# Two network layers on one core: the second tile's mask and exponentials a step earlier, both scalings in one step, and a new order at the seams

## The chip, the core and the metric

The kernel runs on one core of a Trainium2 chip. Its engines are TensorE (PE, matrix products), VectorE (DVE), ScalarE (ACT), GpSimd (POOL) and SyncE (SP, which here issues every DMA). The metric is the device time of one execution in microseconds; lower is better. Each engine works through its own instructions in the order in which the program gives them, and waits on semaphores where an instruction needs another engine's result or a buffer that another engine still reads.

## The reference

Input are 128 graphs of 64 nodes with 768 features each (`x`) and their adjacency (`adj`). Two layers follow each other, each with a residual and a layer norm. Cut to what matters:

```python
# layer 0, 12 heads of 64
h = einsum('bnd,ade->bane', x, W);  th = tanh(h)
attn = (th . w_src) + transpose(th . w_dst)
attn = where(attn >= 0, attn, 0.2 * attn)
attn = softmax(where(~adj, -999.0, attn))
f = elu(attn @ h + b)
g = sigmoid(x @ H_w.T + H_b)
x = layernorm(x + g * f + (1 - g) * x)
# layer 1, 6 heads of 128
q, k, v = x @ Wq + bq, x @ Wk + bk, x @ Wv + bv
p = softmax(where(adj, q @ k.T / sqrt(128), -9e15))
x = layernorm(x + (p @ v) @ Wf + bf)
```

Everything is in 32-bit floats.

## The kernel before, in words

The 8192 rows are 64 tiles of 128 rows (two graphs each), and two tiles make a pair; there are 32 pairs. **Phase A** computes layer 0 and the V product of layer 1; **phase B** computes Q, K, the attention and the output product of layer 1, for 16 groups of two pairs. Nothing is left to a scheduler: both phases collect closures in a table `events` with `at(step, ...)`, and `run` calls them step by step. A step is therefore a place in the order of every engine, not a time. Within a step the closures stand in the order in which they were entered: older pairs first, and within a pair tile 1 before tile 0.

**The products of phase A.** Each product of a pair (`W`, `G` for the gate, `V`) is done in seven steps with pre-added blocks in place of eight (class `Product`, `mms` at L209); a step is three products of 128x128 by 128x384, which PE runs as six instructions. The blocks of the weights are added once (L173 and L167), those of the tokens for each pair on POOL (`token_sums`, L258 to L261) after DVE has transposed the tiles (`turn`, L395). Steps 0, 2 and 3 leave a snapshot of a PSUM bank in SBUF on ACT (`snap`, L416), since the bank goes on being accumulated: step 2 adds to the bank of step 0, step 4 to that of step 2, step 5 to that of step 3. Steps 1, 4 and 5 are taken out on DVE by an addition with a snapshot (L439 for W and G, L458 for V), step 6 by a copy on ACT (L437, L456). Step 6 adds to the bank that step 4's addition has read. In the steady part a pair `p` begins at step `o = 21 p - 21`: W at `o` to `o + 6`, G at `o + 7` to `o + 13`, and at `o + 14` to `o + 20` the V product of pair `p - 3`.

**A tile of layer 0** (class `Tile0`; the profile's lines are given). Tile 1 counts its steps from `s = o`, tile 0 from `s = o + 5`.

- `tanh` (ACT L475) and `cap`; `dst_mul` and `src_mul` (POOL L479, L487); `dst_sum` (DVE L482 and a transpose L484) and `src_sum` (DVE L491).
- `dst_out` (four DMAs, L497) writes the sums to DRAM, and `dst_in` (two DMAs, L505) reads them back spread over the partitions, into `s`. `exchange` (L515, L516) swaps halves of `h`.
- `add`: twelve Prelus on ACT (L529), in two halves. `mask` (DVE L536) and `top` (a maximum, DVE L540). `exp`: twelve exponentials on ACT with their sums (L545), in two halves.
- `scale`: per half a reciprocal on DVE (L553) and a product on POOL (L555).
- `probs`: six transposes on PE (L566) in two halves, each copied by ACT into `pt` (L571). `aggregate`: PE L584. `elu`: DVE L605, then `e` on ACT (L612), in a second use of the buffer `pt`.
- `mix1`, `mix2`: DVE L616, L617, L625, L626. `norm1`: statistics on DVE (L284, L293, L295), a power and two small products on POOL (L296, L298, L299). `norm2`: one pass on ACT (L303). `spill`: a DMA.
- `gate_in` (POOL L594) and `gate` (ACT L598) work on the gate.

**The end of phase A.** The last pair starts at `o = O[-1]`. No W or G follows it; the V products of pairs 29, 30 and 31 stand at `o + 21`, `o + 28` and `o + 45`. The last needs both tiles of pair 31 transposed, which PE does at `o + 42` and `o + 43` (L410, copies L411). Phase B's first weights are loaded from `o + 7` on; the 14 sums of the blocks of `Wq` run on POOL, one a step from `o + 22`, and those of `Wk` on DVE from `o + 36` (L167).

**Phase B.** A product over a group takes 15 steps (table `STEPS`, class `Stream`), each of two products of 128 by 128 by 256 (L866). They need eleven sums of token blocks (`group_sum`, L836, list `SUMS`; `SUM_STEPS` tells at which step each is used). The results accumulate through first copies on ACT (L887) and additions on DVE (L892 for q and k, L909 for the output product). A sum that names an index of 6 or more uses an earlier sum. For group 0 all sums stand ahead of its first product, two of three on DVE and the third on POOL; for group 1 every second one is on DVE; later groups have them on POOL.

**The end of the kernel.** The last pair's output gets its statistics by block (`end_stats`, L1039); `end_norm` then does for tile 1, and after it for tile 0: L1043 and L1045 on DVE, the power on POOL (L1046), two passes on DVE (L1049) each followed by a store (L1050).

Of the kernel before, what the change touches and what calls it, by code (L numbers as in the profile page):

```python
# [9 lines left out]
F32 = mybir.dt.float32  # L10
U8 = mybir.dt.uint8
AF = mybir.ActivationFunctionType
ALU = mybir.AluOpType
# [48 lines left out]
def kernel(  # L62
# [221 lines left out]
        nc.vector.bn_stats(st[:, half, :], r[:, halves(half)])  # L284
        return st

    def layernorm(small, r, eps):
        st = layernorm_half(small, r, None, 0)
        return layernorm_rest(small, layernorm_half(small, r, st, 1), eps)

    def layernorm_rest(small, st, eps):
        mv = small.tile([P, 2], F32, name="mv")
        nc.vector.bn_aggr(mv, st.rearrange("p a s -> p (a s)"))  # L293
        rstd = small.tile([P, 1], F32, name="rstd")
        nc.vector.tensor_scalar_add(rstd, mv[:, 1:2], eps)  # L295
        nc.gpsimd.tensor_tensor(rstd, rstd, neg_half, ALU.pow)  # L296
        shift = small.tile([P, 1], F32, name="shift")
        nc.gpsimd.tensor_tensor(shift, mv[:, 0:1], rstd, ALU.mult)  # L298
        nc.gpsimd.tensor_tensor(shift, shift, neg_one, ALU.mult)  # L299
        return rstd, shift  # L300

    def normalize(r, rstd, shift):
        nc.scalar.activation(r, r, AF.Identity, bias=shift, scale=rstd)  # L303


    def phase_a(ctx):
# [160 lines left out]
        class Tile0:  # L467
            def __init__(self, p, i):
                self.p, self.i, self.d = p, i, st[p]
                self.sd = sds[i]  # L470

            def tanh(self):
                self.h = self.d["h"][self.i]
# [126 lines left out]
            def elu(self):  # L600

                self.z = k3.tile([P, D], F32, name="z")
                zv = self.z.rearrange("p (j h e) -> p j h e", h=2, e=E)
                for h2 in range(2):
                    nc.vector.tensor_tensor(  # L605
                        zv[:, :, h2, :],
                        self.pos[h2],
                        b_bc[:, None, :].to_broadcast([P, A // 2, E]),
                        ALU.add,
                    )  # L610
                self.e = k3.tile([P, D], F32, name="pt")
                nc.scalar.activation(self.e, self.z, AF.Exp, bias=neg_one)  # L612

            def mix1(self):
# [11 lines left out]
                nc.vector.scalar_tensor_tensor(xt, xt, 4.0, e, op0=ALU.mult, op1=ALU.add)  # L626

            def norm1(self):
                self.stats = layernorm(small, self.d["x"][self.i], 4.0 * EPS)

            def norm2(self):
                xt = self.d["x"][self.i]
                normalize(xt, *self.stats)

            def spill(self):
# [30 lines left out]
        for p in range(NP):  # L666
            d, o = st[p], O[p]
            d["p"] = p
            if p:
                at(max(o - 20, 1), lambda p=p: load_adj(p))  # L670
                at(o + 8, lambda p=p: load(p))

            def xb_in(d, i):
                d.setdefault("xp", []).append(blocks(x_t[2 * d["p"] + i]))

            def xT(d, i):
                d.setdefault("T", []).append(turn(d["xp"][i]))

            if p:
                at(max(o - 20, 1), lambda d=d: xb_in(d, 0))  # L680
                at(max(o - 16, 1), lambda d=d: xb_in(d, 1))
                at(o - 6, lambda d=d: xT(d, 0))
                at(o - 5, lambda d=d: xT(d, 1))
                at(o - 4, lambda d=d: sums(d))
            else:
                at(0, lambda d=d: d.update(T=[transposed(t) for t in d["x"]]))
                at(0, lambda d=d: sums(d))
            at(o, lambda d=d: start_h(d))
            at(o + 7, lambda d=d: start_g(d))
            for i in range(7):  # L690
                at(o + i, lambda d=d, i=i: dense(d, "W", i))
                at(o + 7 + i, lambda d=d, i=i: dense(d, "G", i))
            for i, s in ((1, o), (0, o + 5)):
                t = Tile0(p, i)
                at(s + 6 + (i == 0), t.tanh, t.cap)
                at(s + 7, t.dst_mul)
                at(s + 8, t.src_mul)
                at(s + 9, t.dst_sum, t.dst_out)
                at(s + 10, t.src_sum)
                at(s + 13, t.dst_in)  # L700
                at(s + 16, t.exchange)

                at(s + (15 if i else 17), lambda t=t: t.add(0))
                at(s + (16 if i else 17), lambda t=t: t.add(1))
                at(o + (14 if i else 16), t.gate_in)
                at(o + (17 if i else 18), t.gate)
                at(s + 18, t.mask, t.top)
                at(s + 19, lambda t=t: t.exp(0))

                at(s + (19 if i else 20), lambda t=t: t.exp(1))  # L710
                at(s + 21, lambda t=t: t.scale(0))
                at(s + 22, lambda t=t: t.scale(1))
                at(s + 24, t.probs)
                at(s + 25, t.aggregate)
                at(s + 26, t.elu)
                at(s + 27, t.mix1)
                at(s + 28, t.mix2)
                at(s + 29, t.norm1)
                at(s + 30, t.norm2)
                at(s + 31, t.spill)  # L720

            def x1_in(d, i):
                d["xp", i] = blocks(x1_d[2 * d["p"] + i])

            def x1T(d, i, t):
                d["x1T", i] = t
                nc.sync.dma_start(xT_d[d["p"]][:, i], t)

            def x1_sums(d):
                d["T"] = [d["x1T", i] for i in range(2)]  # L730
                sums(d)

            if p < NP - 3:
                v = O[p + 3] + 14
                times = ((1, v - 19, v - 13), (0, v - 16, v - 10))
            elif p < NP - 1:

                v = O[-1] + (21 if p == NP - 3 else 28)
                times = ((1, v - 16, v - 7), (0, v - 15, v - 6)) if p == NP - 3 else (
                    (1, v - 12, v - 7), (0, v - 10, v - 6)  # L740
                )
            if p < NP - 1:
                for i, t0, t1 in times:
                    at(t0, lambda d=d, i=i: x1_in(d, i))
                    at(t1, lambda d=d, i=i: x1T(d, i, turn(d["xp", i])))
                at(times[1][2] + 1, lambda d=d: x1_sums(d))
            else:
                v = o + 45
                for i in range(2):
                    at(o + 43 - i, lambda d=d, i=i: x1T(d, i, transposed(d["x"][i])))  # L750
                at(o + 44, lambda d=d: x1_sums(d))
            at(v, lambda d=d: start_v(d))
            for i in range(7):
                at(v + i, lambda d=d, i=i: dense(d, "V", i))
# [14 lines left out]
            at(o + (7 + k if k < 4 else 8 + 2 * k), lambda k=k: load_early(0, Wq, k))  # L769
            at(o + 20 + 2 * k, lambda k=k: load_early(1, Wk, k))  # L770
        for k in range(len(WEIGHT_SUMS)):
            at(o + 22 + k, lambda k=k: weight15_sum(early[0], k, nc.gpsimd))
            at(o + 36 + k, lambda k=k: weight15_sum(early[1], k, nc.vector))
        at(o + 30, lambda: load_T4(0))
        run(events, O[-1] + 80)
# [3 lines left out]
    def phase_b(ctx, wq, wk):  # L779
# [258 lines left out]
                d["e", i] = k1.tile([P, 3, 6], F32, name=f"est{i}")  # L1038
            nc.vector.bn_stats(d["e", i][:, nb], d["x", 1, i][:, nb * 256 : (nb + 1) * 256])  # L1039

        def end_norm(g, d, i):
            mv = small.tile([P, 2], F32, name="mv")
            nc.vector.bn_aggr(mv, d["e", i].rearrange("p a s -> p (a s)"))  # L1043
            rstd = small.tile([P, 1], F32, name="rstd")
            nc.vector.tensor_scalar_add(rstd, mv[:, 1:2], EPS)  # L1045
            nc.gpsimd.tensor_tensor(rstd, rstd, neg_half, ALU.pow)  # L1046
            for half in range(2):
                r = d["x", 1, i][:, halves(half)]
                nc.vector.tensor_scalar(r, r, mv[:, 0:1], rstd, op0=ALU.subtract, op1=ALU.mult)  # L1049
                nc.sync.dma_start(out_t[4 * g + 2 + i][:, halves(half)], r)  # L1050
# [17 lines left out]
        for g in range(NG):  # L1068
# [6 lines left out]
            ready = {}  # L1075
            for k in range(len(SUMS)):

                eng = nc.vector if (k % 3 != 2 if g == 0 else g == 1 and k % 2) else nc.gpsimd
                if g == 0:
                    group_sum(d, k, eng)  # L1080
                    continue
                if g == 1:

                    t = max([R * 3 + SUM_STEPS[k] + 1] + [ready[r] for r in SUMS[k][:2] if r in ready])
                    ready[6 + k] = t
                else:
                    t = o - 24 + 2 * k
                at(t, lambda d=d, k=k, eng=eng: group_sum(d, k, eng))
# [15 lines left out]
            for q in range(2):  # L1104
# [37 lines left out]
                    at_first(f + i, lambda d=d, q=q, i=i: d["F", q].step(i))  # L1142
                if last and q:
                    for b in range(6):
                        t = f + 1 + max(i for i in range(R) if STEPS[i][5][b])
                        at(t, lambda d=d, b=b: end_stats(d, b))
                    for i in (1, 0):
                        at(f + R, lambda g=g, d=d, i=i: end_norm(g, d, i))
                    continue
                for i in range(2):  # L1150
                    t = f + R + 1 + 2 * i
# [48 lines left out]
```

## Time and profile before

| | |
|---|---|
| device time, median of 3 runs | 2919.01 us (2911.96 to 2919.04) |
| the profiled execution | 2916.2 us |
| its span | 2914.4 us |
| PE, PEld, DVE, ACT, POOL busy | 97, 71, 62, 41, 53% of the span |
| first matmul after | 5.99 us |
| phase A's last product ends, phase B's first begins | about 1510 us |
| granted clock of PE, mean | 0.995 |

A row of a timeline gives start and length in us, engine, line, operation, output and inputs, how many instructions were merged, and in brackets the idle time before it with what ended it. A row of the waits gives who waited for whom, the total in us, how often, and the longest wait. Times are from the start of the span. Ends of matmuls are modelled, so the distance between starts says more than the length of a row.

### The profile page before, as it was taken

The numbers are of one execution on the slowest core, as the hardware profiler recorded it, in microseconds if no ns is written. First come the engines' busy times: TensorE is split into PE (matmuls) and PEld (weight loads), VectorE is DVE, ScalarE is ACT, GpSimd is POOL, SyncE is SP. The second block draws the span as 40 slices with busy tenths as digits, with TensorE's granted clock in tenths as the row PEclk, the third lists the DMA queues.
The fourth block names the chain that finished last, engine by engine and source line by source line (L and its number), as shares of the span: only waits on it lengthen the run. The fifth ranks groups of instructions, "written<-read, shape, count | busy, mean of one in ns | idle before, by whom it ended". The sixth has DMA issues, their size and how long they took to land.

```text
span 2914.4 us, 50727 instructions
## 1 busy us (share of the span) xinstructions
PE 2838.2 (97%) x18108; PEld 2062.3 (71%) x18108; DVE 1820.1 (62%) x3710; ACT 1203.7 (41%) x3739; POOL 1554.4 (53%) x1641
## 2 busy tenths in 40 slices
PE   8899999999999999999989999999999999999998
PEld 4455555555555555555558888888888888888887
DVE  4876766767667677676775555555555555555556
ACT  3666566565665656656532212222211222211223
POOL 3755555556555555555563554455454455454455
PEclk9999999999999999999999999999999999999999
DMA  6434344453443544435560212122212212212222
GB/s 167 112 109 142 119 139 134 123 151 116 140 131 118 152 121 136 136 119 145 160 201 27 71 61 77 62 82 88 73 59 77 80 64 88 83 57 69 88 82 71
DMA packets 358683, 308.40 MB, mean 106 GB/s; under 512 B 226592, under 2 KB 304160, under 8 KB 358432
## 3 DMA queue, kind: packets, MB, share of 16 engines
q1 hardware_dynamic: 358432, 305.16, 34.1%
q8 instruction: 144, 2.36, 0.3%
q14 instruction: 107, 0.88, 0.1%
HBM read 191.41 MB, written 101.06 MB: 100 GB/s over the span
## 4 chain that ended last, share of the span: by engine, by line
PE 74%; ACT 10%; DVE 9%; POOL 4%; issue 2%; DMA 1%; SPq 1%; DVEq 0%; ACTq 0%; POOLq 0%
PE X L866 42%; PE X L209 25%; ACT s L545 4%; PE pb L1006 2%; POOL s L555 2%; DVE s L536 2%; ACT s L529 2%; PE pa L584 2%; PE pb L931 2%; ACT snap L416 1%; PE pa L566 1%; DVE pt L616 1%; DVE pt L617 1%; ACT pt L612 1%; DVE nmx L540 1%
## 5 line engine op out<-in xcount | busy, mean ns | idle before, releaser
L209 PE MATMUL X<-w,S 128*128 128x384 f32 x2304 | 799.2, 492 | 26.4 <-ACT snap L416 14.9
L866 PE MATMUL X<-S,w 128*128 128x256 f32 x2816 | 665.1, 382 | 3.7 <-DVE q L892 2.4
L209 PEld LDWEIGHTS X<-w,S 128*128 128x128 f32 x2304 | 428.0, 190 | 322.7 <-issue 30.8
L209 PE MATMUL X<-w,T 128*128 128x384 f32 x1728 | 600.8, 491 | 4.4 <-DMA w<-in_L_gnn_W_dram 2.5
L866 PEld LDWEIGHTS X<-S,w 128*128 128x128 f32 x2816 | 524.8, 190 | 76.8 <-DVE q L892 2.8
L209 PEld LDWEIGHTS X<-w,T 128*128 128x128 f32 x1728 | 328.9, 192 | 229.8 <-ACT snap L416 8.5
L848 POOL TENSOR_TENSOR Sc<-cT 128x256 f32<-128x256 f32 x224 | 161.6, 728 | 405.1 <-PE X L866 388.1
L866 PE MATMUL X<-w,Sc 128*128 128x256 f32 x1408 | 322.5, 381 | 1.0 <-DVE xs L909 0.8
L909 DVE TENSOR_TENSOR xs<-xs,X 128x256 f32<-128x256 f32 x512 | 210.8, 420 | 169.6 <-PE X L866 160.9
L545 ACT ACTIVATE s<-s,nmx 128x64 f32<-128x64 f32 x768 | 256.1, 335 | 128.4 <-DVE nmx L540 128.4
L866 PEld LDWEIGHTS X<-w,Sc 128*128 128x128 f32 x1408 | 265.5, 190 | 38.6 <-DVE xs L909 1.6
L892 DVE TENSOR_TENSOR k<-k,X 128x256 f32<-128x256 f32 x320 | 133.6, 421 | 217.8 <-PE X L866 167.6
L555 POOL TENSOR_TENSOR s<-s,rs 128x384 f32<-128x384 f32 x128 | 128.5, 1004 | 225.2 <-DVE rs L553 122.2
L892 DVE TENSOR_TENSOR q<-q,X 128x256 f32<-128x256 f32 x320 | 133.3, 420 | 184.0 <-PE X L866 149.3
L866 PE MATMUL X<-xb,w 128*128 128x256 f32 x960 | 236.6, 379 | 0.0
L303 ACT ACTIVATE xs<-xs,shift,rstd 128x768 f32<-128x768 f32 x62 | 63.5, 1025 | 417.8 <-POOL shift L299 409.7
L887 ACT ACTIVATE k<-X,bk_c 128x256 f32<-128x256 f32 x192 | 91.0, 474 | 304.5 <-PE X L866 304.5
L887 ACT ACTIVATE q<-X,bq_c 128x256 f32<-128x256 f32 x192 | 91.1, 474 | 282.5 <-PE X L866 282.5
L416 ACT COPY snap<-X 128x384 f32<-128x384 f32 x288 | 136.3, 473 | 172.8 <-PE X L209 170.8
L479 POOL TENSOR_TENSOR tmp<-th,wd_bc 128x768 f32<-128x768 f32 x64 | 137.6, 2150 | 122.6 <-ACT th L475 122.6
L866 PEld LDWEIGHTS X<-xb,w 128*128 128x128 f32 x960 | 181.2, 190 | 24.0
L529 ACT ACTIVATE s<-s,src 128x64 f32<-128x64 f32 x768 | 193.5, 339 | 4.8 <-DMA s<-dst_d 4.8
(118 smaller groups left out, 4026.4 us busy)
## 6 DMA issues: line engine op xcount, KB each, us to landing
xb<-in_x_dram SPq DMA_DIRECT2D x64, 384.0 KB
s<-dst_d SPq DMA_DIRECT2D x128, 192.0 KB
x_d<-xb SPq DMA_DIRECT2D x64, 384.0 KB
xT_d<-T SPq DMA_DIRECT2D x64, 384.0 KB
v_d<-v SPq DMA_DIRECT2D x128, 192.0 KB
xb<-xT_d SPq DMA_DIRECT2D x32, 768.0 KB
xb<-v_d SPq DMA_DIRECT2D x256, 96.0 KB
xs<-x_d SPq DMA_DIRECT2D x64, 384.0 KB
```

The lines of the kernel that those rows point to most:

```text
L209: nc.tensor.matmul(o, self.lhsT(i, c), rhs, start=first and c == 0, stop=last and c == CH - 1, skip_group_check=True,)
L303: nc.scalar.activation(r, r, AF.Identity, bias=shift, scale=rstd)
L416: nc.scalar.copy(t, ps)
L479: nc.gpsimd.tensor_tensor(self.tmp, self.th, wd_bc, ALU.mult)
L529: nc.scalar.activation(self.s[:, a], self.s[:, a], AF.Prelu, bias=self.src[:, a : a + 1], alpha=LEAKY_ALPHA,)
L545: nc.scalar.activation(self.s[:, a], self.s[:, a], AF.Exp, bias=self.nmx[:, a : a + 1], accum_out=self.sm[:, a : a + 1],)
L555: nc.gpsimd.tensor_tensor(t, t, rs[:, :, None].to_broadcast([P, A // 2, S]), ALU.mult)
L848: nc.gpsimd.tensor_tensor(t, pair_part(d, q, r0), pair_part(d, q, r1), op)
L866: nc.tensor.matmul(ps, self.lhsT(r, slot, c), self.rhs(r, slot, c), start=start and c == 0, stop=stop and c == 1, skip_group_check=True,)
L887: nc.scalar.activation(o[:, b], ps, AF.Identity, bias=bias[:, hd : hd + 1], scale=1.0 if positive else -1.0)
L892: nc.vector.tensor_tensor(o[:, b], o[:, b], ps, ALU.add if positive else ALU.subtract)
L909: nc.vector.tensor_tensor(o, o, ps, ALU.add if positive else ALU.subtract)
```

## The change

Seven edits, all in the order of the work or in where it is done.

1. Tile 1's `mask`, `top` and first half of `exp` stand one step earlier in all pairs (`n = s - 1`; the second half keeps its step). Tile 0 keeps its steps.
2. `scale(0)` and `scale(1)` stand in one step, for both tiles.
3. In the last pair tile 0 counts from `o + 3`, not `o + 5`.
4. In the last pair `e` uses the buffers `th` and `tmp`, not `pt`, and `norm2` is one pass on DVE with mean and power, in place of two small products on POOL and a pass on ACT.
5. The 14 sums of the `Wq` blocks stand two a step from `o + 21`.
6. Group 0's sums are all on DVE; the first four stand ahead of the products, the others up to four steps ahead of their use. In group 1 other six sums are on DVE, so that no sum on DVE needs one from POOL.
7. At the end the statistics stand a step earlier, and the first part of `end_norm` becomes `end_top`, which is done for both tiles before the passes, tile 1's a step before tile 0's.

```diff
-    def layernorm_rest(small, st, eps):
+    def layernorm_rest(small, st, eps, plain=False):
         mv = small.tile([P, 2], F32, name="mv")
         nc.vector.bn_aggr(mv, st.rearrange("p a s -> p (a s)"))
         rstd = small.tile([P, 1], F32, name="rstd")
         nc.vector.tensor_scalar_add(rstd, mv[:, 1:2], eps)
         nc.gpsimd.tensor_tensor(rstd, rstd, neg_half, ALU.pow)
+        if plain:
+            return mv[:, 0:1], rstd
...
+                self.last = p == NP - 1
...
-                self.e = k3.tile([P, D], F32, name="pt")
+
+                self.e = k3.tile([P, D], F32, name=("th", "tmp")[self.i] if self.last else "pt")
...
             def norm2(self):
                 xt = self.d["x"][self.i]
+                if self.last:
+                    mean, rstd = self.stats
+                    nc.vector.tensor_scalar(
+                        xt, xt, mean, rstd, op0=ALU.subtract, op1=ALU.mult
+                    )
+                    return
                 normalize(xt, *self.stats)
...
-            for i, s in ((1, o), (0, o + 5)):
+            for i, s in ((1, o), (0, o + (3 if p == NP - 1 else 5))):
...
-                at(s + 18, t.mask, t.top)
-                at(s + 19, lambda t=t: t.exp(0))
-
-                at(s + (19 if i else 20), lambda t=t: t.exp(1))
-                at(s + 21, lambda t=t: t.scale(0))
-                at(s + 22, lambda t=t: t.scale(1))
+                n = s - (i == 1)
+                at(n + 18, t.mask, t.top)
+                at(n + 19, lambda t=t: t.exp(0))
+                at(n + 20, lambda t=t: t.exp(1))
+                at(s + 21, lambda t=t: t.scale(0), lambda t=t: t.scale(1))
...
-            at(o + 22 + k, lambda k=k: weight15_sum(early[0], k, nc.gpsimd))
+            at(o + 21 + k // 2, lambda k=k: weight15_sum(early[0], k, nc.gpsimd))
...
-        def end_norm(g, d, i):
+        def end_top(d, i):
...
+            d["n", 1, i] = mv, rstd
+
+        def end_norm(g, d, i):
+            mv, rstd = d["n", 1, i]
...
-                eng = nc.vector if (k % 3 != 2 if g == 0 else g == 1 and k % 2) else nc.gpsimd
+
+                eng = nc.vector if g == 1 and k in (2, 3, 5, 6, 8, 10) else nc.gpsimd
                 if g == 0:
-                    group_sum(d, k, eng)
+
+                    t = max(min(SUM_STEPS[k], *(
+                        [SUM_STEPS[m] - 1 for m in range(len(SUMS)) if 6 + k in SUMS[m][:2]] or [99]
+                    )) - 4, -1)
+                    if t < 0:
+                        group_sum(d, k, nc.vector)
+                    else:
+                        at(t, lambda d=d, k=k: group_sum(d, k, nc.vector))
                     continue
...
-                        t = f + 1 + max(i for i in range(R) if STEPS[i][5][b])
+                        t = f + max(i for i in range(R) if STEPS[i][5][b])
                         at(t, lambda d=d, b=b: end_stats(d, b))
-                    for i in (1, 0):
-                        at(f + R, lambda g=g, d=d, i=i: end_norm(g, d, i))
+
+                    at(f + R - 2, lambda d=d: end_top(d, 1))
+                    at(f + R - 1, lambda d=d: end_top(d, 0))
+                    at(f + R - 1, lambda g=g, d=d: end_norm(g, d, 1))
+                    at(f + R - 1, lambda g=g, d=d: end_norm(g, d, 0))
```

More of the change, by code (lines that the diff above doesn't have):

```diff
@@ L285, in layernorm_half, with layernorm @@
         return st
-    def layernorm(small, r, eps):
+    def layernorm(small, r, eps, plain=False):
         st = layernorm_half(small, r, None, 0)
-        return layernorm_rest(small, layernorm_half(small, r, st, 1), eps)
-    def layernorm_rest(small, st, eps):
+        return layernorm_rest(small, layernorm_half(small, r, st, 1), eps, plain)
+    def layernorm_rest(small, st, eps, plain=False):
         mv = small.tile([P, 2], F32, name="mv")
@@ L628, in norm1 @@
             def norm1(self):
-                self.stats = layernorm(small, self.d["x"][self.i], 4.0 * EPS)
+                self.stats = layernorm(small, self.d["x"][self.i], 4.0 * EPS, self.last)
             def norm2(self):
                 xt = self.d["x"][self.i]
+                if self.last:
[4 more added lines that the diff above has]
+                    return
                 normalize(xt, *self.stats)
```

## The prediction

> **What bounds the kernel now.** I read the page's parts 1 and 2, then the table of stages, the waits and the timelines of single engines. Busy time, and TensorE's (PE's) share of each of 40 slices (72.9 us each):
>
> ```profile
> PE 2838.2 (97%) x18108; PEld 2062.3 (71%) x18108; DVE 1820.1 (62%) x3710; ACT 1203.7 (41%) x3739; POOL 1554.4 (53%) x1641
> PE   8899999999999999999989999999999999999998
> ```
>
> PE is full except at the start, at slice 20 (the seam between the phases) and at the end. By stage (us, PE, PEld, DVE, ACT, POOL busy, clock, DMA):
>
> ```profile
> 200.00:1430.00 1230.00, 1209.89 (x6392) 719.54 (x6391) 863.59 (x1417) 746.57 (x2599) 700.22 (x655) 1.00 0.45 132
> 1430.00:1600.00 170.00, 155.20 (x918) 114.32 (x917) 105.54 (x186) 56.60 (x156) 86.58 (x75) 0.98 0.40 127
> 1600.00:2880.00 1280.00, 1279.82 (x9804) 1108.26 (x9803) 697.62 (x1845) 286.51 (x595) 637.48 (x781) 1.00 0.22 73
> 2880.00:2915.00 35.00, 25.59 (x160) 21.35 (x158) 21.93 (x63) 4.48 (x5) 18.21 (x31) 0.93 0.25 90
> ```
>
> Phase B from 1600 on idles 0.2 us: nothing is to be had there. Steady phase A idles 20 us, the seam 15, the end 9. All of steady phase A's waits of PE (200 to 1430 us; total, times, longest):
>
> ```profile
> PE X L209 <- ACT snap L416: 11.4, 27, 0.4
> PE pa L566 <- POOL s L555: 8.7, 28, 0.3
> ```
>
> Two waits, once in each pair of tiles. One pair, PE first, then who is late:
>
> ```profile
> 819.29 4.03 PE L209 MATMUL X<-w,T 128*128 128x384 f32 x12
> 823.75 2.17 PE L209 MATMUL X<-w,S 128*128 128x384 f32 x6 [0.43 <-ACT snap L416]
> 837.15 0.49 PE L566 MATMUL pa<-ident,s 128*128 128x128 f32 x3
> 837.96 0.55 PE L566 MATMUL pa<-ident,s 128*128 128x128 f32 x3 [0.31 <-POOL s L555]
> ```
> ```profile
> 816.17 1.53 DVE L536 TENSOR_TENSOR s<-s,cap 128x768 f32<-128x768 f32 x1
> 823.14 0.47 ACT L416 COPY snap<-X 128x384 f32<-128x384 f32 x1
> 836.06 0.18 DVE L553 RECIPROCAL rs<-sm 128x6 f32<-128x6 f32 x1
> 836.38 1.52 POOL L555 TENSOR_TENSOR s<-s,rs 128x384 f32<-128x384 f32 x1 [2.22 <-DVE cap L522]
> ```
>
> A matmul of 384 columns starts every 0.3225 us (18 from 809.62 to 815.42). Twelve from 819.29 end at 823.16; the next starts at 823.75, 0.59 late, and its six take 0.07 longer: **0.66 us** for a shown wait of 0.43, since the pipeline empties. Likewise three transposes at 0.109 end at 837.48, and the next starts at 837.96: **0.48**. The first is W's step 2, waiting for the snapshot of step 0, which stands on ACT behind tile 1's 12 exponentials (818.78 to 822.78). The second waits for scale(1) of tile 0, whose reciprocal stands on DVE behind mix1. A pair takes 45.26 us (823.75 to 869.01).
>
> **What the Trainium skill says.** "SBUF — State Buffer", section "Who interferes with whom": a DVE operation with two SBUF inputs and a POOL operation that reads SBUF exclude each other; the first to start keeps the port. The trace agrees: the mask L536 takes 1.53 us above beside a POOL sum (L261, then 1.72), and 0.96 at 826.52, without one. "TensorE: Matmul & The Clock Gate", section "What's actually happening": after an idle window of about 3.4 us PE runs at half clock until it has been busy for as long. The trace agrees: after the wait of 4.69 us at 187.52 six matmuls take 4.18 us, against 2.10.
>
> **The change part by part.**
>
> (a) *Tile 1's mask and exponentials a step sooner, steady pairs.* Nothing is added or removed. The Prelus end at 813.68, the transposes ahead of the mask at 813.7. The mask moves ahead of the eviction of V's step 4 (L458 at 815.69): 813.75 to 814.7 if it gets the port first (POOL's L258 started at 813.85), 815.75 if second; the maximum (0.95) ends at 815.7 to 816.7. The eviction behind it (0.56) ends by 817.3 at worst; V's step 6 wants it at 817.36: free, with no margin at the worst end. On ACT twelve exponentials (4.0) and tile 0's gate (0.75) follow, end at 820.5 to 821.5, then V's last copy (0.36) and the snapshot (0.38): ready by 821.8 to 822.3 against 823.16. 0.66 goes, 27 times: 17.8.
>
> (b) *Both scalings in one step.* Tile 0's second reciprocal goes ahead of mix1: exponentials done at 832.83 or earlier, POOL scales by about 834.7, PE wants them at 837.5. 0.48 goes, 28 times: 13.4. Tile 1's second reciprocal makes DVE wait for the exponentials in front of two transposes; W's first addition behind them is wanted only after 823.2, so nothing.
> Sum of (a) and (b): **-31.2**. If mask, maximum and eviction end 0.4 us too late, 28 x 0.4 comes back: -20.
>
> (c) *First four pairs (60 to 200 us).* The same two waits are larger there: POOL s 7.6 in 5 and 4.7 once, DVE 3.5 in 2 (mix1 ahead of mask and eviction), ACT about 3, and half clock after them. But the copies of the probabilities wait for mix2 (L571 at 87.72 and 126.62), which moves little: of the wait at 86.87 I keep 2.3, of 123.30 and 127.27 with the slow clock 4.2, of 100.86 and 143.09 2.4; at 187.52 mix and norm of the old pair still come first: 1.6. 10.5 with little for the snapshots; each is unsteady, I take **-9** (-3 to -15).
>
> (d) *The last pair.* Before, tile 0's transposes wait 6.37 us for the norm:
>
> ```profile
> 1493.60 1.55 PE L410 MATMUL pa<-ident,xb 128*128 128x128 f32 x6 [6.37 <-ACT xb L303]
> ```
> Tile 0 moves two steps up (3.9 us of PE); two shifts on POOL and an ACT pass (1491.70 to 1493.5) become one DVE pass (0.87, as two of L1049); e no longer holds `pt`. Against it: **SP** issues tile 0's four dst_out ahead of tile 1's two dst_in (before at 1433.65): they wait for sdT, ready at 1439 to 1441, so dst_in goes out at 1442 to 1443.6, and lands about 3 us later (issue ending 1455.51, first Prelu 1458.59). Tile 1's Prelus start 1.5 to 4 late, with V's snapshot behind them. **ACT**: tile 0's 12 Prelus (2.97) go ahead of the snapshot of pair 29's V, step 0, for which its step 2 waits: 1.03 becomes 2.4 to 3. **POOL**: eight weight sums (1.27 each alone, 1.55 to 1.75 beside DVE) now lie between tile 0's scale and tile 1's pow: 10 to 14 us, pow at 1482 to 1488; DVE's new pass for tile 1 waits for it in front of tile 0's mix (3.9), norm (1.5 to 2) and pass. Tile 0's transposes then come at 1491 to 1496.5 instead of 1493.60; 1.14 of that was counted in (a, b), and the last product's eviction, behind DVE's weight sums that start later, costs 0.8: -0.7 to +4.8. I take **+2**.
>
> (e) *First group.* Before:
>
> ```profile
> 1518.36 1.13 PE L866 MATMUL X<-S,w 128*128 128x256 f32 x4 [2.36 <-DVE q L892]
> 1568.53 1.13 PE L866 MATMUL X<-xs,w 128*128 128x256 f32 x4 [1.54 <-DVE k L892]
> ```
> At 1518 an accumulator waits behind sums on DVE, slowed by POOL's (1.2 to 1.75 each, 0.6 alone). All go to DVE, without POOL beside them, and only seven precede the first L892: 4.3 us from 1509.83, when step 5 needs it at 1514.9. 2.5 of start-to-start delay and 0.8 at 1512.26 go. For group 1 DVE's sums no longer need POOL's (1.16 us wait at 1567.45): 1.7. Sum **-5** (-3.5 to -5.5).
>
> (f) *End.*
>
> ```profile
> 2910.50 0.87 DVE L1049 TENSOR_SCALAR xs<-xs,mv,rstd 128x384 f32<-128x384 f32 x2 [0.66 <-POOL rstd L1046]
> ```
> Tile 1's statistics end a step before, both pows run beside DVE, four passes of 0.43 close at about 2909.8 instead of 2911.37. Four stores then come closer together. **-1.4** (-0.8 to -1.6).
>
> Sum: -31.2 - 9 + 2 - 5 - 1.4 = **-44.6**. The profiled execution took 2916.2 (span 2914.4), 2.8 under the median of 2919.0; taken from the median: **2874.4**.
>
> **Rivals.**
> 1. *A new wait in place of the old*: mask and maximum hold V's eviction, or the snapshot stays late by less: half of (a, b) is lost, +15: 2889. For it: the mask took 1.98 at 1449.69 beside POOL. Against: the mask starts first by the times above. 0.18.
> 2. *Absorbed*: DVE and ACT, now nearer to their turns, meet waits of equal length elsewhere, and what (c, e, f) bring goes to (d): 2915. Against: DVE is busy for 70% of a steady pair, ACT 61%. 0.05.
> 3. *Slower*: the mask, in DVE's order ahead of V's eviction, waits for Prelus that come late as the pair shortens (the round trip through dst_d). Behind it stand both V evictions; V's step 6 and all after it wait. It decides if the Prelus end some 0.6 us later than now; to lose over 0.3% it must cost 1.9 us a pair: 28 x 2 - 44.6 = +11: 2930. Against: dst_in is issued at 1433.65 in a like pair and used at 1442.71, 8 us in hand. 0.06.
> The forecast has 0.71.
>
> About 0.3%, 8.8 us, is what a measurement of this kernel can tell from no change. Faster takes the forecast, rival 1 and a little of 2: 0.90; same 0.05; slower 0.05. Bounds of the terms: -55 to -22. With rival 1 inside the range: **2861 to 2896**.
>
> **What would show it.** Right: between 200 and 1400 us PE waits for neither snap nor scale, and a pair takes 44.1 us. At the seam, pow of tile 1 stands behind L167, and L410 still waits. At 1518 and 1568 the waits are gone. Wrong: a steady wait of PE with X released by DVE v L458 or ACT v L456 (rival 1), or DVE L536 waiting for ACT s L529 by more than a microsecond (rival 3).

## The result: 2913.3 us, no change that can be told

The changed kernel takes 2913.33 us (median of 4 runs, 2910.81 to 2915.58) against 2917.2 of the kernel before (2911.96 to 2919.04): a ratio of 0.9989 (95% interval 0.9972 to 1.0007). Forecast were 2874.4, 2861 to 2896. The profiled execution took 2912.64 us, its span is 2910.7.

The page's busy times, and two rows of the table of stages (us, PE, PEld, DVE, ACT, POOL busy, clock, DMA):

```profile
PE 2831.1 (97%) x18108; PEld 2067.9 (71%) x18108; DVE 1852.5 (64%) x3716; ACT 1206.6 (41%) x3737; POOL 1510.3 (52%) x1633
```
```profile
200.00:1430.00 1230.00, 1199.43 (x6385) 723.47 (x6383) 892.39 (x1414) 751.98 (x2597) 660.49 (x650) 1.00 0.45 132
1430.00:1600.00 170.00, 160.06 (x933) 117.42 (x932) 106.14 (x195) 54.41 (x155) 81.48 (x73) 0.98 0.41 127
```

In steady phase A PE's shown idle time didn't fall from 20 to 0 us: it rose to 30.6. DVE is busy 29 us longer there and POOL 40 us less, though the change gives neither of them more or less to do in a steady pair: the time in which an instruction is held up is in these sums, as in the 2.57 us of L629 below. All waits of PE from 200 to 1430 us are one row, and it is neither of the two that stood there:

```profile
PE pa L587 <- ACT pt L574: 30.6, 28, 1.4
```

Both old waits are gone, as forecast. A new one stands at tile 0's aggregate (L587, before L584), which waits for ACT's copies of the probabilities (L574, before L571). The page's chain that ended last names who is behind ACT:

```profile
PE X L875 42%; PE X L209 33%; DVE pt L629 3%; PE pa L587 2%; PE pb L1015 2%; PE pb L940 2%; DVE pt L620 2%; DVE xb L630 1%; DVE pt L621 1%; ACT pt L616 1%; DVE z L608 1%; PE pb L995 1%; ACT s L548 1%; PE pa L569 1%; ACT pt L574 0%
```

L629, the first operation of `mix2`, is the longest link outside PE's products. The timelines of the pair around 835 us, DVE, POOL, then ACT and PE of the changed kernel:

```profile
832.91 1.58 DVE L620 SCALAR_TENSOR_TENSOR pt<-pt,z 128x768 f32<-128x768 f32 x1
834.52 0.96 DVE L621 SCALAR_TENSOR_TENSOR pt<-pt,xb 128x768 f32<-128x768 f32 x1
835.53 2.57 DVE L629 SCALAR_TENSOR_TENSOR pt<-gp,pt 128x768 f32<-128x768 f32 x1
838.13 0.96 DVE L630 SCALAR_TENSOR_TENSOR xb<-xb,pt 128x768 f32<-128x768 f32 x1
```
```profile
832.05 1.62 POOL L558 TENSOR_TENSOR s<-s,rs 128x384 f32<-128x384 f32 x2 [2.14 <-issue]
835.43 1.85 POOL L482 TENSOR_TENSOR tmp<-th,wd_bc 128x768 f32<-128x768 f32 x1 [1.76 <-ACT th L478]
```
```profile
834.51 0.85 ACT L478 ACTIVATE th<-hp 128x768 f32<-128x768 f32 x1
839.18 0.86 ACT L574 COPY pt<-pa 128x384 f32<-128x384 f32 x2 [2.63 <-DVE xb L630]
839.71 0.27 PE L587 MATMUL pa<-hp,pt 64*64 64x64 f32 x1 [1.08 <-ACT pt L574]
```

And the kernel before in the same place (DVE, then POOL, then ACT):

```profile
834.19 0.96 DVE L616 SCALAR_TENSOR_TENSOR pt<-pt,z 128x768 f32<-128x768 f32 x1
836.26 0.95 DVE L625 SCALAR_TENSOR_TENSOR pt<-gp,pt 128x768 f32<-128x768 f32 x1
837.25 1.47 DVE L626 SCALAR_TENSOR_TENSOR xb<-xb,pt 128x768 f32<-128x768 f32 x1
```
```profile
836.38 1.52 POOL L555 TENSOR_TENSOR s<-s,rs 128x384 f32<-128x384 f32 x1 [2.22 <-DVE cap L522]
837.86 2.52 POOL L479 TENSOR_TENSOR tmp<-th,wd_bc 128x768 f32<-128x768 f32 x1
```
```profile
835.79 0.85 ACT L475 ACTIVATE th<-hp 128x768 f32<-128x768 f32 x1
838.80 0.86 ACT L571 COPY pt<-pa 128x384 f32<-128x384 f32 x2 [0.97 <-DVE xb L626]
```

Read the starts. Before, POOL's second scale came 0.12 us after L625. DVE kept the port (the one whose rule the prediction cites), and POOL's product was the one that stretched, 0.83 to 1.52. POOL's next, `dst_mul`, stood behind it until 837.86. Now both scalings are done by 833.7, so POOL is free when the tanh ends, and `dst_mul` (L482) starts at 835.43, 0.10 us ahead of `mix2` (3.23 us behind DVE's last addition of W's step 5, at 832.20; before 4.38, from 833.48). Now DVE is second: L629 takes 2.57 in place of 0.95.

That lead of 0.10 has two sources. Counted from DVE's addition of W's step 5, the tanh ends at the same place in both kernels (3.16 us), and before, POOL wasn't free then; now it is. But `mix2` also starts later than before, at 3.33 in place of 2.78: the first operation of `mix1` (L620) now starts while POOL is scaling and takes 1.58 in place of 0.96.

The rest follows from the buffer. `mix2` ends at 839.09. Tile 1's `e` lies in the one buffer `pt` until then, and tile 0's probabilities are to be copied into that buffer: the copies start at 839.18. PE has done its transposes and six matmuls and would start the aggregate at 838.56 (836.53 + 2.03); it starts at 839.71. With 0.1 more until the next product that is 1.25 us a pair: 44.06 without this wait (own_e below), 45.31 with it.

Places in the traces, us: the first aggregate; from there to tile 0's aggregate of the fourth pair; one steady pair (mean of 20); from pair 30's last aggregate to phase B's first product.

| kernel | whole, median | ratio (95%) | first | first four pairs | a pair | last pair |
|---|---|---|---|---|---|---|
| before | 2917.2 | | 75.3 | 131.5 | 45.25 | 81.9 |
| changed | 2913.3 | 0.9989 (0.9972-1.0007) | 73.0 | 132.3 | 45.31 | 82.2 |
| early_only | 2895.3 | 0.9926 (0.9914-0.9939) | 72.4 | 126.2 | 44.59 | 83.5 |
| scale_only | 2940.0 | 1.0083 (1.0069-1.0097) | 73.4 | 135.0 | 45.99 | 84.3 |
| seams_only | 2916.8 | 0.9998 (0.9990-1.0006) | 73.6 | 131.7 | 45.26 | 87.4 |
| own_e | 2883.0 | 0.9881 (0.9868-0.9895) | 74.5 | 133.0 | 44.06 | 83.3 |
| tanh_later | 2881.6 | 0.9882 (0.9867-0.9897) | 76.1 | 131.2 | 44.06 | 82.1 |
| own_e_split | 2898.3 | 0.9936 (0.9923-0.9948) | 72.9 | 129.4 | 44.57 | 88.5 |
| own_e_split4 | 2878.5 | 0.9870 (0.9856-0.9883) | 72.7 | 129.2 | 44.09 | 83.2 |
| own_e_oldlast | 2885.8 | 0.9895 (0.9882-0.9909) | 73.0 | 133.3 | 44.06 | 86.9 |
| combined | 2877.3 | 0.9861 (0.9843-0.9879) | 77.4 | 128.1 | 44.06 | 82.1 |

The first aggregate moves by 1.7 us between the kernel before and seams_only, and by 4.9 between early_only and combined, though in each of these two cases the order of the work up to there is the same. So the column "first" is no effect of an edit, and the spans of two single profiled executions are not compared as wholes.

### The profile page after: what moved, and what is told of

Its sections match the earlier page's. It is cut to its first block, busy times and chain, and to the rows that moved or that the text cites. A ratio compares the mean times of both kernels' runs of the same rounds, so it can differ in the third digit from the quotient of the medians.

```text
span 2910.7 us, 50738 instructions
## 1 busy us (share of the span) xinstructions
PE 2831.1 (97%) x18108; PEld 2067.9 (71%) x18108; DVE 1852.5 (64%) x3716; ACT 1206.6 (41%) x3737; POOL 1510.3 (52%) x1633
## 4 chain that ended last, share of the span: by engine, by line
PE 82%; DVE 11%; ACT 3%; issue 1%; POOL 1%; SPq 1%; DMA 1%; DVEq 0%; POOLq 0%; ACTq 0%
PE X L875 42%; PE X L209 33%; DVE pt L629 3%; PE pa L587 2%; PE pb L1015 2%; PE pb L940 2%; DVE pt L620 2%; DVE xb L630 1%; DVE pt L621 1%; ACT pt L616 1%; DVE z L608 1%; PE pb L995 1%; ACT s L548 1%; PE pa L569 1%; ACT pt L574 0%
## 5 line engine op out<-in xcount | busy, mean ns | idle before, releaser
L875 PEld LDWEIGHTS X<-S,w 128*128 128x128 f32 x2816 | 525.0, 190 | 73.6 <-DVE S L845 1.5
L482 POOL TENSOR_TENSOR tmp<-th,wd_bc 128x768 f32<-128x768 f32 x64 | 120.9, 1889 | 145.1 <-ACT th L478 145.1
L296 POOL TENSOR_TENSOR rstd<-rstd,neg_half 128x1 f32<-128x1 f32 x126 | 69.1, 548 | 235.7 <-DVE rstd L295 235.4
```

Of the source, the lines that this page charges most:

```text
L482: nc.gpsimd.tensor_tensor(self.tmp, self.th, wd_bc, ALU.mult)
L875: nc.tensor.matmul(ps, self.lhsT(r, slot, c), self.rhs(r, slot, c), start=start and c == 0, stop=stop and c == 1, skip_group_check=True,)
```

## The experiments

**own_e: pt freed of e.** On the changed kernel, `e` is written over the tile's own probabilities `s`, which have been read by then:

```diff
-                self.e = k3.tile([P, D], F32, name=("th", "tmp")[self.i] if self.last else "pt")
+                if self.last:
+                    self.e = k3.tile([P, D], F32, name=("th", "tmp")[self.i])
+                else:
+                    self.e = self.s.rearrange("p a m -> p (a m)")
```


> The changed kernel, but e is written over the tile's own probabilities (buffer s, read out by then) and no longer over pt; the last pair keeps th and tmp. Theory (the copies of the probabilities wait for mix2 of the other tile, since e held pt, and mix2 is late behind POOL's products): the wait of the aggregate L587 for the copies L574 goes, 1.1 us shown in each of 28 pairs, 1.2 with the refill; a steady pair takes 44.1 us in place of 45.31, the whole 2913 - 34 = about 2879. Rival (the pair is bound by DVE and POOL together, and any wait taken away comes back at the next place): a new wait of about the same length at L569, L209 or L587, a pair of 45.0 to 45.3, the whole 2905 to 2914.

Measured 2883.0, a pair 44.06, and no wait at L587 in the steady part. All waits of PE from 200 to 1430 us are now one, once, and that one lies in the last pair (at 1419.30):

```profile
PE X L209 <- ACT snap L418: 3.6, 1, 3.6
```
L629's counterpart L632 still takes 2.57 (at 821.34), but nothing waits for it: the copies of the probabilities no longer stand behind it. The rival falls: nothing else came in the wait's place. The whole is 4 us above what was expected. The steady pairs brought the 34 us; against the changed kernel's trace 1.5 us are lost before the first aggregate, 0.7 in the first four pairs, 1.1 in the last pair and 1.2 in phase B.

**The two main edits apart.** Edit 1 alone, and edit 2 alone, on the kernel before:

```diff
-                at(s + 18, t.mask, t.top)
-                at(s + 19, lambda t=t: t.exp(0))
-                at(s + (19 if i else 20), lambda t=t: t.exp(1))
+                n = s - (i == 1)
+                at(n + 18, t.mask, t.top)
+                at(n + 19, lambda t=t: t.exp(0))
+                at(n + 20, lambda t=t: t.exp(1))
```
```diff
-                at(s + 21, lambda t=t: t.scale(0))
-                at(s + 22, lambda t=t: t.scale(1))
+                at(s + 21, lambda t=t: t.scale(0), lambda t=t: t.scale(1))
```

> The kernel before with edit 1 alone (tile 1's mask, maximum and first exponentials a step sooner). Theory: the wait of W's step 2 for the snapshot goes and nothing takes its place, since scale and mix keep their order: a pair takes 44.6 us in place of 45.26, the whole 2917 - 18 = about 2899, and the wait of the transposes for POOL's scale stays (0.3 shown). Rival (any wait taken away comes back): 2914 to 2919, with a longer wait at the transposes or the aggregate.

> The kernel before with edit 2 alone (both scalings in one step). Theory: tile 0's scale wait (0.31 shown) goes, but both of its POOL products now stand beside mix1, and POOL's next product (dst_mul) takes the port ahead of mix2: mix2 ends later, the copies of the probabilities wait for pt, and the aggregate L584 waits 0.4 to 1.1 us for them: a pair of 45.2 to 45.9 in place of 45.26, the whole 2915 to 2935. Rival (what the prediction said, the scale's wait goes and nothing comes): a pair of 44.8, the whole 2917 - 13 = 2904.

Waits of PE from 200 to 1430 us, early_only and then scale_only:

```profile
PE pa L566 <- POOL s L555: 8.3, 27, 0.3
```
```profile
PE pa L584 <- ACT pt L571: 29.6, 27, 1.4
PE X L209 <- ACT snap L416: 10.9, 25, 0.5
```

Edit 1 alone takes 0.66 us off a pair and makes the kernel 0.74% faster. Edit 2 alone adds 0.74 to a pair and makes it 0.83% slower: it exchanges its 0.48 for the wait at the aggregate. Together they cancel, 45.31 against 45.25. In scale_only the same two lines meet (POOL L479 at 848.00, DVE L625 at 848.10 for 2.57), with `mix1` again at 1.58 in front of them, so the collision is edit 2's own and needs no help from edit 1. early_only's pair came out at the 44.6 that was expected; scale_only's lies just above its expected range (45.2 to 45.9), and so does its whole, 2940.0 against 2915 to 2935.

**seams_only: edits 3 to 7.** The changed kernel with both of the diffs above undone.

> The changed kernel without edits 1 and 2: the seams' edits 3 to 7 alone. From the two traces' landmarks (start of phase B against the last steady aggregate +0.3 us, first groups -3.1, end -1.0): 2917 - 4 = about 2913, with a steady pair of 45.26 and both of its waits as before. Rival (the seams bring what the prediction said, -5 - 1.4 + 2 and less): 2911 to 2912; or the order of the last pair costs more than the table shows: 2916 or more.

2916.8: no gain. The first group and the end keep what they brought (5.28 us for the first 24 instructions of phase B, as in the changed kernel), but the last pair takes 87.4 us in place of 81.9. There tile 0's second scale again stands in a step of its own, now behind POOL's two weight sums a step, and PE waits for it (1430 to 1600 us):

```profile
PE pa L569 <- POOL s L558: 4.8, 2, 4.1
```

The third case of the expectation held. With edit 5's weight sums in place, the last pair's new order needs edit 2; without edit 5 it was not run.

**tanh_later: the port alone.** One line, `pt` shared as before:

```diff
-                at(s + 6 + (i == 0), t.tanh, t.cap)
+                at(s + 7, t.tanh, t.cap)
```


> The changed kernel with one line changed: tile 1's tanh and cap a step later (s + 7), so that on ACT the tanh stands behind a snapshot and POOL's dst_mul L482 starts some 2 us later, after mix2; e still shares pt. Theory (dst_mul, started 0.1 us ahead of mix2's first operation, took the port and stretched it from 0.95 to 2.57; that alone makes pt late): L629 takes 0.95 again, mix2 ends about 1.6 us sooner, the aggregate waits no more, a steady pair takes 44.1 to 44.2, the whole 2913 - 31 = about 2882. Rival (the port isn't it, the place of mix2 behind the longer mix1 is): L629 or L630 stay long and the aggregate's wait stays above 0.5: 45.0 or more, the whole above 2900.

DVE, POOL and ACT of tanh_later, the same place in the same pair:

```profile
821.14 0.96 DVE L629 SCALAR_TENSOR_TENSOR pt<-gp,pt 128x768 f32<-128x768 f32 x1
822.13 0.96 DVE L630 SCALAR_TENSOR_TENSOR xb<-xb,pt 128x768 f32<-128x768 f32 x1
```
```profile
823.00 1.91 POOL L482 TENSOR_TENSOR tmp<-th,wd_bc 128x768 f32<-128x768 f32 x1 [3.70 <-ACT th L478]
```
```profile
822.07 0.85 ACT L478 ACTIVATE th<-hp 128x768 f32<-128x768 f32 x1
823.18 0.86 ACT L574 COPY pt<-pa 128x384 f32<-128x384 f32 x2 [0.26 <-DVE xb L630]
```

The tanh stands behind a snapshot, `dst_mul` starts when `mix2` is done, both of `mix2`'s operations take 0.96, and the copies come in time. 44.06 a pair, 2881.6 us. `mix1` in front of it (L620) is still stretched to 1.58 by the scalings, as in the changed kernel: that alone costs PE nothing. `dst_mul` itself comes 2 us later (end at 824.91); DVE's sum of it (L485) starts at 824.99, still directly behind the work ahead of it, so nothing is lost. Either end of the chain, the port or the buffer, undoes the loss when it alone is taken away.

**What edit 2 is worth with pt free.**

```diff
-                at(s + 21, lambda t=t: t.scale(0), lambda t=t: t.scale(1))
+                at(s + 21, lambda t=t: t.scale(0))
+                at(s + 22, lambda t=t: t.scale(1))
```
(own_e_split; in own_e_split4 the second line has `s + (22 if p < 4 else 21)`.)

> own_e with the two scalings in two steps again, as before the change: what edit 2 is worth once pt is free. Theory (the wait for the second scale is 0.48 a pair, as the prediction said): a steady pair of 44.54 in place of 44.06, but the first four pairs (to the aggregate of 207 us in own_e) end some 6 to 8 us sooner, as with edit 1 alone: the whole 2883 + 13 - 7 = about 2889. Rival (the first pairs lose for another reason than edit 2): 2896.

> own_e with the scalings in two steps in the first four pairs alone. Theory: the steady pair of 44.06 with the first pairs 6 to 8 us sooner: about 2876. Rival (the first pairs lose for another reason): 2882 to 2884.

A steady pair of 44.57 against 44.06: the scale's wait was worth 0.5, as the prediction had it. own_e_split missed its 2889 by 9. Of that about 5 is the last pair, which takes 88.5 us in it, for the reason of seams_only, which the expectation forgot; over 3 is that the first four pairs gain 3.6 us and not about 7. In own_e_split4 they gain 3.7 us and the whole 4.5, also less than expected (6 to 8).

Why edit 2 costs in the first pairs is the same lock, but the way from there to PE depends on where `e` lies. In the changed kernel it is `pt` again: from 60 to 207 us the aggregates wait 5.8 us for the copies (3 times), and in early_only not at all. In own_e it is `s`. POOL, then DVE, the DMA queue of SP and ACT of own_e:

```profile
82.53 2.52 POOL L482 TENSOR_TENSOR tmp<-th,wd_bc 128x768 f32<-128x768 f32 x1
85.13 2.40 POOL L490 TENSOR_TENSOR th<-th,ws_bc 128x768 f32<-128x768 f32 x1
```
```profile
83.41 2.45 DVE L632 SCALAR_TENSOR_TENSOR s<-gp,s 128x768 f32<-128x768 f32 x1
85.90 2.45 DVE L633 SCALAR_TENSOR_TENSOR xb<-xb,s 128x768 f32<-128x768 f32 x1
```
```profile
88.49 1.15 SPq L508 DMA_DIRECT2D s<-dst_d  x2
92.55 1.54 ACT L532 ACTIVATE s<-s,src 128x64 f32<-128x64 f32 x6 [7.88 <-DMA s<-dst_d]
```

POOL's products and `mix2` take turns, and `mix2` ends at 88.35. It reads `e`, which now lies in `s`, so `dst_in` (L508), which fills `s` anew, has to wait for that end (SP's waits of 60 to 100 us have it in 2, the longest of 8.1): it goes out at 88.49. The Prelus wait 7.88 us for it, and PE waits 5.95 for a snapshot behind them (at 96.86). In own_e_split4 the second operation of `mix2` takes 1.47, `dst_in` goes out at 85.18 and the Prelus start at 89.18; 1.8 of these 3.3 us are the earlier start of that execution. So own_e frees one buffer by holding another. In the steady pairs that costs nothing (PE waits for nothing there), in the first ones it does: in the changed kernel, where `e` lies in `pt`, the like `dst_in` is issued at 78.72.

**own_e_oldlast: the last pair as before.** On own_e; with `self.last` false, the norm has its shifts on POOL and its pass on ACT, and `e` lies over `s` here too.

```diff
-                self.last = p == NP - 1
+                self.last = False
...
-            for i, s in ((1, o), (0, o + (3 if p == NP - 1 else 5))):
+            for i, s in ((1, o), (0, o + 5)):
```

> own_e with the last pair as before the change (edits 3 and 4 undone). Theory (the prediction's +2 for the last pair, and 82 us from the last steady aggregate to phase B's first product before against 83.3 in own_e): 1 to 2 us faster than own_e, about 2881.5. Rival (the last pair's new order saves something): 2884 or more.

2.8 us slower than own_e, 86.9 us in place of 83.3 in the last pair: the rival was right, with edits 2 and 5 in place in both. The two intervals (0.9868 to 0.9895 and 0.9882 to 0.9909) just overlap, so the sign rests on the trace.

**combined: a version that beats both kernels.** On the changed kernel:

```diff
-                at(s + 6 + (i == 0), t.tanh, t.cap)
+                at(s + 6 + (i == 0 or p > 4), t.tanh, t.cap)
...
-                at(s + 21, lambda t=t: t.scale(0), lambda t=t: t.scale(1))
+                at(s + 21, lambda t=t: t.scale(0))
+                at(s + (22 if p < 4 else 21), lambda t=t: t.scale(1))
```

> The changed kernel with the scalings in two steps in the first four pairs, and tile 1's tanh and cap a step later from pair 5 on; e shares pt as before. Theory (the first pairs as with edit 1 alone, 199 to 202 us to the first steady aggregate; then 27 intervals of 44.06; seams and end as in the kernel with the later tanh): about 2874. Rival (the first pairs' gain is lost again at the last pair): 2879 to 2882.

2877.3, the lowest median, though not told apart from own_e_split4 (2878.5). Its profiled execution had the latest first aggregate of all (77.4), with an order up to there that is early_only's (72.4); from there the first four pairs took 128.1 us, against 132.3 in the changed kernel.

## Why the prediction was wrong, step by step

Differences of start times between the two traces, which add up to the span's -3.7 us:

| term | forecast | measured in the changed kernel |
|---|---|---|
| (a, b) steady pairs | -31.2 | +1.8 |
| (c) start and first four pairs | -9 | -1.5, of it +0.8 after the first aggregate |
| (d) last pair | +2 | +0.3 |
| (e) first groups | -5 | -3.1 |
| (f) end, with phase B | -1.4 | -1.2, of it -0.9 after the last matmul |

**(a) was right**, in mechanism and size. The mask starts at 813.09 and takes 0.96; it got the port, and POOL's L258 took 1.65. W's step 2 starts at 822.55 and waits for nothing. Alone it brings 0.66 a pair, which is what was worked out.

**(b) is the step that failed.** It was put at -13.4; edit 2 alone costs 0.74 a pair, about +20 over 27 pairs. That the scale's 0.48 would go was right. That nothing would take its place was not. The prediction put the second reciprocal ahead of `mix1` and followed POOL's scale to its end at 834.7, and stopped there. By its own times that scale lies across the start of `mix1` (834.19 before), whose stretch to 1.58 it put at nothing. Nor did it ask what POOL would do next with its freed time: `dst_mul`, at the very moment of `mix2`. And it didn't list who waits for `mix2`: the copies into `pt`. In the trace before, the copies stood at 838.80 with `[0.97 <-DVE xb L626]`, so they were already waiting for `mix2`, only 0.7 us ahead of where PE would feel it. The pieces were in the text: the Trainium skill's rule on the port ("SBUF — State Buffer", "Who interferes with whom": the first to start keeps it), and in (c) the sentence that the copies of the probabilities wait for `mix2`. They weren't put together for the steady pair. The trace agrees with the rule to a tenth of a microsecond: where POOL came 0.12 behind, POOL stretched; where it came 0.10 ahead, DVE did. (In the prediction's own example the sum that held the mask is L260, started at 815.89; L261, which it names, stood behind the mask.)

The lower bound of (a, b), -20 with mask, maximum and eviction 0.4 too late, bounded the wrong thing: it took in errors of the steps that were followed, not a wait that none of them named.

**Rival 2** ("DVE and ACT meet waits of equal length elsewhere", 2915) is what happened in the steady pairs, though it had only 0.05; its second half, that (d) eats what the ends bring, is not: (d) took 0.3, and (e) and (f) kept 4.3. Rival 1 had a new wait too, but half of the loss and another place. Against rival 2 stood that DVE is busy for 70% of a steady pair. That share doesn't bear on it: the loop is PE's product, L441, `mix1`, `mix2`, copies, aggregate, and its length counts in that one place.

**(c)** failed by the same lock, on the path shown under own_e_split4. Edit 1 alone brought 5.3 us in the first four pairs, edit 2 alone cost 3.5, and both together brought nothing.

**(d)** lay within its range (-0.7 to +4.8), but not by the steps that were summed, so the hit is partly luck. Held: tile 1's power stands behind the weight sums at 1486.74 (forecast 1482 to 1488), and tile 0's transposes come at 1495.28 (1491 to 1496.5). Not held: those transposes wait for nothing, where the prediction's sign was that L410 (now L412) still waits, and the snapshot of pair 29's V is waited for 1.14 us, 1.30 from start to start (forecast 2.4 to 3). The 6.37 of before is gone, and this has come in its place (1430 to 1600 us):

```profile
PE X L209 <- ACT snap L418: 6.3, 3, 2.9
1487.11 3.65 PE L209 MATMUL X<-w,S 128*128 128x384 f32 x6 [2.94 <-ACT snap L418]
```

Besides the 1.14, PE waits 2.21 at 1449.87 for a snapshot of pair 28's V, which stands behind tile 1's late Prelus: the prediction had seen that delay, but named no wait of PE for it. And it waits 2.94 for one of pair 30's V, which on ACT stands behind tile 0's `e`. That `e` waits for `elu`, which on DVE stands behind tile 1's `mix1` and `mix2`, of 1.83 to 1.91 an operation beside POOL's weight sums; the prediction named none of this. After each of these two waits the granted clock falls (0.55 and 0.59 over the next 3.8 and 3.4 us), and six matmuls take 3.73 and 3.44 from start to start in place of 1.94. Both waits are shorter than the idle window of 3.4 us that the prediction goes by; here the measurement decides. The likeliest value was too dark: with edits 2 and 5 in place, the old order is the slower one (own_e_oldlast).

**(e)** is half right. The 2.5 and 0.8 at the first group went: from phase B's first product to its 25th instruction 8.74 became 5.28. The 1.7 at group 1 didn't go. Waits of PE there (1430 to 1600 us):

```profile
PE X L875 <- DVE k L901: 1.7, 2, 1.5
```
POOL is no longer what holds DVE; DVE's own sums are. From 1563.27 to 1565.79 a fill (1.20 us) and two sums (0.68, 0.69) stand ahead of the addition that PE wants. The prediction took away the reason named in the trace and didn't ask what was late next.

**(f)** was right: the time from the last matmul's start to the end fell by 0.9 (8.42 to 7.48), within -0.8 to -1.6, and the four passes (L1062 at 2905.78) now follow each other without a wait.

## What to carry to other kernels

When an edit finishes an engine's work earlier, write down that engine's next instruction and the moment at which it will now start: here a POOL product that could start 1.2 us sooner took the port 0.1 us ahead of a DVE operation, which the same edit had put back by 0.55, and cost more than the edit brought. Then list who waits for each instruction that may stretch, buffers included; a row that already shows a wait for it (0.97 on ACT here), though PE doesn't feel it, is the place with the least margin. Two edits made together can cancel: each done alone showed -0.7% and +0.8% where the pair showed nothing.

## What was not expected of the hardware

In these traces a lead of a tenth of a microsecond decided which engine paid, and the second paid for nearly all that was left of the first: a DVE operation of 0.95 us that started 0.10 behind a POOL product of 1.85 took 2.57, while POOL's product was not stretched. The other way round, POOL's product of 0.83 that started 0.12 behind DVE took 1.52, and the next one, of 1.85, took 2.52 beside DVE's L626, which itself went to 1.47. In the first pairs, where both engines have work in a row, both sides stretched: 2.40 to 2.52 on POOL, 2.45 on DVE.
